# One set of row transposes for the maxima of two head groups in a four-batch decoder layer

## The chip, the cores and the metric

The kernel runs on one core of a Trainium2 chip. Times are device microseconds (us) of that core; lower is better. The engines are TensorE (PE, matrix products and transposes), VectorE (DVE), ScalarE (ACT), GpSimd (POOL) and SyncE (SP, which issues most transfers). They run side by side, each through its own queue in order, and wait for each other through semaphores.

## The reference

A pre-norm decoder layer on x of shape 4 x 512 x 512, all in float32:

```python
x = x + self_attention(layernorm(x))      # 16 heads of 32, causal, q/k/v/o weights and biases
x = x + cross_attention(layernorm(x), ctx) # 16 heads of 32, keys = values = ctx, no weights,
                                           # causal; masked scores are -10000, not -inf
x = x + ffn(layernorm(x))                  # relu(x Wup) Wdown + (sum of softmaxed top-2 gates) * x Wexpert
```

Both attentions are softmax(q k / sqrt(32)) v. In the cross-attention a masked score takes part in the softmax with the value -10000, so that a row whose largest score is far below zero would still weigh the masked keys.

## The kernel before, in words

The four batches are worked one after another; a batch has 512 rows (4 tiles of 128) and 512 columns (4 tiles of 128). The 16 heads stand in four groups `g` = 0 to 3 of four heads, one group per column tile, head `r` of a group on the 32 partitions from 32 `r`. The order of the work on PE, DVE, ACT and POOL is the order in which the program is written (`tc.manual_schedule` with these four engines); only transfers and the constants made before it are placed by the framework. PSUM is one pool of four buffers of two banks, handed out by `pair`.

One attention (class `Attention`, once per batch for self, once for cross) has two passes:

- `with_maxima` computes the scores with the queries on the partitions, only to find each row's largest score. It has ten units (`units`, counted by `n`), and a unit is one or two pieces of a group. Between the units it lays matmuls of other work (`fill`: projections, feed-forward steps). In `maxima`, a unit's scores are copied out of PSUM by ACT (L308), masked by POOL (L316) and reduced by DVE into `nm`, the negated maxima (L328). Group 0 is complete after unit 2, group 1 after unit 4, groups 2 and 3 after units 7 and 9.
- `attend` computes the scores again, transposed (keys on the partitions, L409), adds the negated maximum of each query by a further small matmul (L420), takes the exponential on ACT (L443), masks on POOL (L451) and multiplies by the values (`values`, `shares`, L486). The product of a unit is written two units behind its scores.

The negated maxima have to lie along a row for L420. `split` writes `nm` (128 x 16 for one group: 4 row tiles, 4 heads) as three bfloat16 parts whose sum is the float32 value, into columns 0, 1 and 2 of each head's 32 columns of a tile `parts`; the other columns are zero. `rows` turns `parts` with four TensorE transposes and copies the result to `mrow` (128 x 512, bfloat16). A product with 32 rows of ones (`onesb`) then adds the three parts up:

```python
lhsT=onesb[h, :],
rhs=self.mrow[g][h, j * P :],
```

There are two `parts` tiles, used alternately (`parts[g % 2]`), and one `mrow` for each group. In `with_maxima` the rows of groups 0 and 1 are turned in units 5 and 7; those of the other groups at its end or in `attend` at unit 3 (`late`). In self-attention groups 2 and 3 are both turned at unit 3 of `attend`, into one PSUM buffer (`mt_s_both`), with two copies by ACT.

The cross-attention also needs the weight of the masked keys. `masked_sums` spreads a group's negated maxima over the partitions with one matmul against `same` (a block matrix of ones, L378, tile `mb`). `masked` takes the exponential on ACT (`ct_c`, L385) and returns `weigh`, three steps (L391 to L393) that multiply by the sums of the later keys' values and by the number of later keys. For groups 0 and 1 the products stand in units 6 and 8, and `weigh` runs on POOL, written right after the scores of units 7 and 9; the others come in `attend`.

The constants (identities, ones, zeroed `parts`) are made by POOL at the start, ahead of the POOL steps of the first layer norm (L208, L210).

Of the kernel before, what the change touches and what calls it, by code (L numbers as in the profile page):

```python
# [18 lines left out]
P = 128  # L19
# [7 lines left out]
def decoder_layer(  # L27
# [37 lines left out]
    def pair(name):  # L65

        return ps.tile([P, 2, S], F32, tag="ps", name=name)
# [96 lines left out]
        allow_small_or_imprecise_dtypes=True,  # L164
    )

    nfloor = const.tile([P, NT, HG], F32, name="nfloor")
    nc.gpsimd.memset(nfloor, -MASKED_BIAS)
    nc.gpsimd.affine_select(
# [7 lines left out]
    )  # L177

    parts = []
    for n in range(2):  # L180
        t = const.tile([P, NT, P], BF16, name=f"parts{n}")
        nc.gpsimd.memset(t, 0.0)
        parts.append(t)
# [86 lines left out]
    class Attention:  # L270
        def __init__(self, q_t, k_t, v, cross, name):
            self.q_t, self.k_t, self.v, self.cross, self.name = q_t, k_t, v, cross, name
            self.nm, self.mrow, self.pv, self.out = {}, {}, {}, None
            self.more, self.sums, self.rden, self.e = {}, {}, {}, None
            self.added = (0, 2) if cross else range(NC - 1)

            self.joined = 1 if cross and name != f"c{B - 1}" else None
            self.joint, self.zero = [], None

        def maxima(self, pieces):  # L280

            at, N = [], 0
            for g, i in pieces:
                at.append(N)
                N += (i + 1) * P
                if g not in self.nm:
                    self.nm[g] = small.tile(
                        [P, NT, HG], F32, tag="nm", name=f"nm_{self.name}_{g}"  # L290
                    )
            name = f"{self.name}_{pieces[0][0]}_{pieces[0][1]}"
            scs = [pair(f"sm_{name}_{n}") for n in range(2)]
            for (g, i), c in zip(pieces, at):
                for r in range(HG):
                    h = slice(r * HD, (r + 1) * HD)
                    nc.tensor.matmul(  # L297
                        scs[r // 2][:, r % 2, c : c + (i + 1) * P],
                        lhsT=self.q_t[h, g, i * P : (i + 1) * P],
                        rhs=self.k_t[h, g, : (i + 1) * P],  # L300
                        start=(c == 0),
                        stop=True,
                        skip_group_check=(c > 0),
                    )
            made = []
            for n in range(2):
                s = work.tile([P, 2, S], F32, tag="pt", name=f"s_{name}_{n}", bufs=6)
                nc.scalar.copy(s, scs[n])  # L308

                if len(pieces) == 1:  # L310
                    diagonal = s[:, :, S - P :].unsqueeze(2)
                elif pieces[0][1] == pieces[1][1]:
                    diagonal = s.rearrange("p u (k q) -> p u k q", k=2)[:, :, :, P:]
                else:
                    diagonal = s[:, :, S - 2 * P :].rearrange("p u (k q) -> p u k q", k=2)
                nc.gpsimd.affine_select(  # L316
                    out=diagonal,
                    in_=diagonal,
                    compare_op=ALU.is_ge,
                    fill=NEG,  # L320
                    base=0,
                    pattern=[[0, 2], [0, len(pieces)], [-1, P]],
                    channel_multiplier=1,
                )
                made.append(s)

            def largest(n, g, i, c):
                nc.vector.tensor_reduce(  # L328
                    self.nm[g][:, i, 2 * n : 2 * n + 2],
                    made[n][:, :, c : c + (i + 1) * P],  # L330
                    axis=AX.X,
                    op=ALU.max,
                    negate=True,
                )

            jobs = [
                (lambda n=n, g=g, i=i, c=c: largest(n, g, i, c))
                for n in range(2)
                for (g, i), c in zip(pieces, at)
            ]  # L340
            if pieces == [(pieces[0][0], NT - 1)]:
                jobs.append(lambda: self.split(pieces[0][0]))
            return jobs

        def split(self, g):

            nm, pt = self.nm[g], parts[g % 2].rearrange("p i (r s) -> p i r s", s=HD)
            if self.cross:
                nc.vector.tensor_tensor(nm, nm, nfloor, ALU.min)
            nc.vector.tensor_copy(pt[:, :, :, 0], nm)  # L350
            rest = small.tile([P, NT, HG], F32, tag="rest", name=f"rest_{self.name}_{g}")
            nc.vector.tensor_tensor(rest, nm, pt[:, :, :, 0], ALU.subtract)
            nc.vector.tensor_copy(pt[:, :, :, 1], rest)
            nc.vector.tensor_tensor(pt[:, :, :, 2], rest, pt[:, :, :, 1], ALU.subtract)

        def rows(self, g, both=None, half=0):


            if both is None:
                tp = ps.tile([P, NT, P], BF16, tag="ps", name=f"mt_{self.name}_{g}")  # L360
            else:
                bank = both[:, 0, :].bitcast(BF16)
                tp = bank[:, half * S : (half + 1) * S].rearrange("p (i q) -> p i q", q=P)
            for i in range(NT):
                nc.tensor.transpose(tp[:, i, :], parts[g % 2][:, i, :], identb)
            self.mrow[g] = work.tile(
                [P, S], BF16, tag="mrow", name=f"mrow_{self.name}_{g}", bufs=4
            )

            def copy(engine=nc.vector.tensor_copy):  # L370
                engine(self.mrow[g], tp.rearrange("p i q -> p (i q)"))

            return [copy]

        def masked_sums(self, g, both=None):

            bc = (pair(f"mb_{self.name}_{g}") if both is None else both)[:, 1, :]
            nc.tensor.matmul(bc, lhsT=same, rhs=self.mrow[g], start=True, stop=True)  # L378
            return g, bc

        def masked(self, g, bc):
# [15 lines left out]
        def scores(self, pieces):  # L397
# [19 lines left out]
            for (g, j), c in zip(pieces, at):  # L417
                for r in range(HG):
                    h = slice(r * HD, (r + 1) * HD)
                    nc.tensor.matmul(  # L420
                        scs[r // 2][:, r % 2, c : c + S - j * P],
                        lhsT=onesb[h, :],
                        rhs=self.mrow[g][h, j * P :],
                        start=False,
                        stop=True,
                        skip_group_check=(len(pieces) > 1),
                    )
# [505 lines left out]
    def run(steps):  # L933
        for step in steps:
            for _ in step() or ():
                pass
# [7 lines left out]
    def with_maxima(steps, a, first=0, norms=()):  # L944
# [17 lines left out]
        for n, pieces in enumerate(units):  # L962
            new = a.maxima(pieces)
            if todo:
                todo.pop()(nc.gpsimd)
            if norms and n % 2 == 0:
                new.append(norms.pop(0))
            due += (total - lead) / len(units)

            count = round(due) - done  # L970
            for k in range(count):
                next(fill, None)
                done += 1
                if k == min(1, count - 1) and n in (5, 7):
                    jobs = a.rows((n - 5) // 2) + jobs
                if k == min(1, count - 1) and a.cross and n in (6, 8):
                    todo.append(a.masked(*a.masked_sums((n - 6) // 2)))
                if n == len(units) - 1 and k == count - (2 if count > 4 else 1):
                    if total >= 2 * len(units):
                        if a.cross:  # L980
                            a.rows(2)[0](nc.scalar.copy)
                    else:
                        late = {3: 2, 5: NC - 1}
                run(jobs[:1])
                jobs = jobs[1:]
            run(jobs)
            jobs = new
        for _ in fill:
            pass
        run(jobs)  # L990
        return late

    def attend(a, late):
# [21 lines left out]
        for n, pieces in enumerate(units):  # L1015
            waiting.append(a.scores(pieces))
            if n in late:
                two = a.cross and late[n] == NC - 1
                together = not a.cross and len(late) == 1
                both = pair(f"mt_{a.name}_both") if two or together else None  # L1020
                copies = a.rows(2, both, 1) if together else []
                copies += a.rows(late[n], both)

                more = [a.masked_sums(2, both)] if two else []
                for copy in copies:
# [13 lines left out]
    with tc.manual_schedule(engines=BY_HAND):  # L1039
# [6 lines left out]
        nc.vector.tensor_reduce(  # L1046
            fold, ident.rearrange("p (c e) -> p e c", e=HD), axis=AX.X, op=ALU.add
        )
        add_bias(e)
        between_self = between_self[1:]  # L1050
        skip, between_cross, ahead = 6, [], []
# [102 lines left out]
```

## Time and profile before

| | |
|---|---|
| median of 3 runs | 790.2 us (790.12 to 790.22) |
| profiled execution, whole | 790.27 us |
| its span, first to last instruction | 788.6 us |
| granted TensorE clock | 1.00 |
| HBM traffic | 30 GB/s over the span |
| POOL select L316 behind ACT copy L308, idle | 100.7 us (cross), 90.0 us (self) |
| DVE maximum L328, 128 calls each | 96.7 us (self), 95.9 us (cross) |

The profile is of one execution. The span is what the profiler sees between the first and the last instruction; the time of the run has 1.7 us more around it. Groups of instructions are listed by source line, engine and operation, with their number, busy time and mean length, and with the idle time ahead of them and what ended it. A chain is the sequence of work that ended last, followed back from the end. Busy time of TensorE counts overlapping matmuls once, and the end of each is modelled; what a matmul holds up is better read from the starts of its neighbours.

### The profile page before, as it was taken

To read this page: it belongs to the slowest core of one execution; us is meant where nothing else is said; L and a number is where in the kernel's file an instruction comes from. 1 tells how busy PE (TensorE), PEld (TensorE's weight loads), DVE (VectorE), ACT (ScalarE), POOL (GpSimd) and SP (SyncE) were. 2 spreads that over 40 slices of the span, in tenths; PEclk is the share of its full clock that TensorE was granted. 3 is DMA by queue.
4 is the path that set the end of the run, shared out by engine and by line. 5 is a ranking of instruction groups with operands and counts; after the bars stand their busy time and mean duration, and the time that the engine had idled before them with its cause. 6 is when DMAs were issued, how large, how long until landed. Compare 5 with 4: busy or idle time off the path is not lost.

```text
span 788.6 us, 14119 instructions
## 1 busy us (share of the span) xinstructions
PE 779.9 (99%) x5484; PEld 369.9 (47%) x5488; DVE 584.2 (74%) x991; ACT 381.7 (48%) x436; POOL 339.8 (43%) x523
## 2 busy tenths in 40 slices
PE   8999999999999999999999999999999999999998
PEld 7444444445444444444544444444544444444444
DVE  2488986988678894498767797698859786989512
ACT  2457516871547505666154741787056814774110
POOL 3434612664234741366233482367323653474100
PEclk9999999999999999999999999999999999999999
DMA  8821400001021300030101130000102030000101
GB/s 290 297 47 27 64 2 1 1 29 54 1 46 25 53 14 1 1 108 28 54 17 35 25 62 1 1 1 2 54 27 81 8 48 0 1 2 2 53 1 53
DMA packets 77779, 31.88 MB, mean 40 GB/s; under 512 B 63504, under 2 KB 67856, under 8 KB 77712
## 3 DMA queue, kind: packets, MB, share of 16 engines
q1 hardware_dynamic: 76992, 30.32, 14.5%
q8 instruction: 43, 0.70, 0.3%
q10 hardware_dynamic: 720, 0.66, 0.2%
q14 instruction: 24, 0.20, 0.1%
HBM read 19.42 MB, written 4.19 MB: 30 GB/s over the span
## 4 chain that ended last, share of the span: by engine, by line
PE 93%; DVE 2%; ACT 2%; issue 2%; DMA 0%; POOL 0%; DVEq 0%
PE pm_qk L245 13%; PE pm_d L233 7%; PE pm_u L245 7%; PE pm_v L233 7%; PE pm_o L764 7%; PE pm_e L233 6%; PE pv_s L486 6%; PE pv_c L486 6%; PE sm_c L297 6%; PE sm_s L297 6%; PE sc_s L409 5%; PE sc_c L409 4%; PE sc_s L420 1%; PE sc_c L420 1%; PE pv_s L562 1%
## 5 line engine op out<-in xcount | busy, mean ns | idle before, releaser
L328 DVE TENSOR_REDUCE nm_s<-s_s 128x2 f32<-128x1024 f32 (+3 forms) x128 | 96.7, 809 | 30.0 <-POOL s_s L316 30.0
L328 DVE TENSOR_REDUCE nm_c<-s_c 128x2 f32<-128x1024 f32 (+3 forms) x128 | 95.9, 810 | 31.0 <-POOL s_c L316 31.0
L308 ACT COPY s_s<-sm_s 128x1024 f32<-128x1024 f32 x80 | 77.1, 1015 | 70.7 <-PE sm_s L297 36.4
L308 ACT COPY s_c<-sm_c 128x1024 f32<-128x1024 f32 x80 | 77.1, 1016 | 35.9 <-PE sm_c L297 16.2
L316 POOL TENSOR_SCALAR_AFFINE_SELECT s_c<-s_c 128x512 f32<-128x512 f32 (+1 forms) x80 | 43.9, 550 | 100.7 <-ACT s_c L308 100.7
L316 POOL TENSOR_SCALAR_AFFINE_SELECT s_s<-s_s 128x512 f32<-128x512 f32 (+1 forms) x80 | 43.7, 550 | 90.0 <-ACT s_s L308 90.0
L556 DVE TENSOR_TENSOR sum_s<-sum_s,pt_s 128x256 f32<-128x256 f32 (+2 forms) x72 | 60.0, 898 | 15.4 <-PE pv_s L486 15.4
L443 ACT ACTIVATE pt_c<-sc_c 128x1024 f32<-128x1024 f32 x64 | 61.8, 1031 | 17.2 <-PE sc_c L420 8.7
L451 POOL TENSOR_SCALAR_AFFINE_SELECT pt_c<-pt_c 128x512 f32<-128x512 f32 (+1 forms) x64 | 53.4, 845 | 20.4 <-ACT pt_c L443 20.2
L233 PE MATMUL pm_d<-wdown_sb,hT 128*128 128x512 f32 x128 | 61.5, 610 | 0.0
L245 PE MATMUL pm_u<-fT,wup_sb 128*128 128x512 f32 x128 | 59.3, 604 | 0.0
L443 ACT ACTIVATE pt_s<-sc_s 128x1024 f32<-128x1024 f32 x56 | 53.9, 1029 | 10.5 <-POOL pt_s L451 5.5
L233 PE MATMUL pm_v<-wv_sb,xnT 128*128 128x512 f32 x128 | 58.8, 600 | 0.0
L245 PE MATMUL pm_qk<-xnT,wk_sb 128*128 128x512 f32 x120 | 57.3, 607 | 0.0
L245 PE MATMUL pm_qk<-xnT,wq_sb 128*128 128x512 f32 x120 | 56.7, 604 | 0.0
L233 PE MATMUL pm_e<-wexp_sb,fT 128*128 128x512 f32 x120 | 56.3, 604 | 0.0
L764 PE MATMUL pm_o<-wo_sb,oT_s 128*128 128x512 f32 x128 | 56.0, 595 | 0.0
L451 POOL TENSOR_SCALAR_AFFINE_SELECT pt_s<-pt_s 128x512 f32<-128x512 f32 (+1 forms) x56 | 48.0, 865 | 16.8 <-ACT pt_s L443 16.2
L409 PE MATMUL sc_c<-cqT,ckT 32*128 32x384 f32 (+3 forms) x512 | 54.1, 464 | 0.9 <-ACT sum_c L443 0.8
L409 PE MATMUL sc_s<-qT,kT 32*128 32x128 f32 (+3 forms) x512 | 54.0, 464 | 0.9 <-ACT sum_s L443 0.9
L671 ACT ACTIVATE kT<-pm_qk,bk_sb 128x512 f32<-128x512 f32 x16 | 11.0, 688 | 85.3 <-PE pm_qk L245 80.7
L297 PE MATMUL sm_c<-ckT,cqT 32*128 32x512 f32 (+3 forms) x512 | 47.5, 460 | 0.0
(172 smaller groups left out, 1291.0 us busy)
## 6 DMA issues: line engine op xcount, KB each, us to landing
cv<-in_ctx_dram SPq DMA_DIRECT2D x16, 256.0 KB, 4.2
cp<-cv SPq DMA_DIRECT2D x64, 64.0 KB, 2.3
out_dram<-x SPq DMA_DIRECT2D x15, 256.0 KB, 2.0
xin<-in_x_dram SPq DMA_DIRECT2D x12, 256.0 KB, 2.7
x<-in_x_dram SPq DMA_DIRECT2D x12, 256.0 KB, 4.4
xnT<-xn_a SPq DMA_DIRECT2D x192, 16.0 KB, 1.8
wv_sb<-in_wv_dram SPq DMA_DIRECT2D x1, 1024.0 KB, 8.3
wo_sb<-in_wo_dram SPq DMA_DIRECT2D x1, 1024.0 KB, 9.9
```

Of the source, the lines that this page charges most:

```text
L233: nc.tensor.matmul(pm, lhsT=lhs_t[:, c, t * P : (t + 1) * P], rhs=w[:, c, :], start=(c == 0), stop=(c == NC - 1),)
L245: nc.tensor.matmul(pm, lhsT=w[:, c, f * P : (f + 1) * P], rhs=rhs_t[:, c, :], start=(c == 0), stop=(c == NC - 1),)
L297: nc.tensor.matmul(scs[r // 2][:, r % 2, c : c + (i + 1) * P], lhsT=self.q_t[h, g, i * P : (i + 1) * P], rhs=self.k_t[h, g, : (i + 1) * P] ...
L308: nc.scalar.copy(s, scs[n])
L316: nc.gpsimd.affine_select(out=diagonal, in_=diagonal, compare_op=ALU.is_ge, fill=NEG, base=0, pattern=[[0, 2], [0, len(pieces)], [-1, P]], ...
L328: nc.vector.tensor_reduce(self.nm[g][:, i, 2 * n : 2 * n + 2], made[n][:, :, c : c + (i + 1) * P], axis=AX.X, op=ALU.max, negate=True,)
L409: nc.tensor.matmul(scs[r // 2][:, r % 2, c : c + S - j * P], lhsT=self.k_t[h, g, j * P : (j + 1) * P], rhs=self.q_t[h, g, j * P :], start= ...
L443: nc.scalar.activation(pt, scs[n], AF.Exp)
L451: nc.gpsimd.affine_select(out=diagonal, in_=diagonal, compare_op=ALU.is_ge, fill=0.0, base=0, pattern=[[0, 2], [0, len(pieces)], [1, P]], ...
L486: nc.tensor.matmul(pv[r * HD : (r + 1) * HD, u, j * P :], lhsT=ones if u else self.v[:, j, h * HD : (h + 1) * HD], rhs=pts[r // 2][:, r % ...
L556: nc.vector.tensor_tensor(to, to, pts[n][:, :, c : c + S - j * P], ALU.add)
L764: nc.tensor.matmul(pms[t // 2][:, t % 2, :], lhsT=a.out[:, c, t * P : (t + 1) * P], rhs=wo_sb[:, c, :], start=(c == 0), stop=(c == NC - 1),)
```

## The change

Groups now have homes: in self-attention groups 0 and 1 share one, and groups 2 and 3; in cross-attention groups 0 and 1 share one, and groups 2 and 3 have one each. The groups of a home share an `nm` tile, one `split` (instructions of 32 columns instead of 16), one set of four transposes and one `mrow`. The second group of a home takes columns 3 to 5 of each head's 32. To pick one group's three rows, the matmul of L420 takes `picks[0]` or `picks[1]` instead of `onesb`, and `masked_sums` takes `sames[0]` or `sames[1]` instead of `same`; these are made once by DVE after the first layer norm. There are four `parts` tiles. The rows of groups 0 and 1 are turned in unit 7, and in the cross-attention both their masked products stand together in unit 8, into the two banks of one PSUM buffer. Their two `weigh` steps come after: one behind the scores of unit 9, the other at the end of `with_maxima`.

```diff
-    for n in range(2):
+    for n in range(4):
         t = const.tile([P, NT, P], BF16, name=f"parts{n}")
         nc.gpsimd.memset(t, 0.0)
...
+            homes = [(0, 1), (2,), (3,)] if cross else [(0, 1), (2, 3)]
+            self.home = {
+                g: (gs, 2 + n - 1 if cross and n else n) for n, gs in enumerate(homes) for g in gs
+            }
...
-            if pieces == [(pieces[0][0], NT - 1)]:
-                jobs.append(lambda: self.split(pieces[0][0]))
+            g = pieces[0][0]
+            if pieces == [(g, NT - 1)] and g == self.home[g][0][-1]:
+                jobs.append(lambda: self.split(g))
...
         def split(self, g):
+            gs, at = self.home[g]
+            N = len(gs)
+            pt = parts[at].rearrange("p i (r s) -> p i r s", s=HD)
+            pt = [pt[:, :, :, k : 3 * N : 3] for k in range(3)]
...
+            nc.vector.tensor_copy(pt[0], nm)
+            nc.vector.tensor_tensor(rest, nm, pt[0], ALU.subtract)
+            nc.vector.tensor_copy(pt[1], rest)
+            nc.vector.tensor_tensor(pt[2], rest, pt[1], ALU.subtract)
...
-            nc.tensor.matmul(bc, lhsT=same, rhs=self.mrow[g], start=True, stop=True)
+            nc.tensor.matmul(bc, lhsT=sames[self.slot(g)], rhs=self.mrow[g], start=True, stop=True)
...
-                        lhsT=onesb[h, :],
+                        lhsT=picks[self.slot(g)][h, :],
...
             if todo:
-                todo.pop()(nc.gpsimd)
+                todo.pop(0)(nc.gpsimd)
...
-                if k == min(1, count - 1) and n in (5, 7):
-                    jobs = a.rows((n - 5) // 2) + jobs
-                if k == min(1, count - 1) and a.cross and n in (6, 8):
-                    todo.append(a.masked(*a.masked_sums((n - 6) // 2)))
+                if k == min(1, count - 1) and n == 7:
+                    jobs = a.rows(0) + jobs
+                if k == min(1, count - 1) and a.cross and n == 8:
+                    both = pair(f"mb_{a.name}_both")
+                    sums = [a.masked_sums(g, both, g) for g in range(2)]
+                    todo.extend(a.masked(*each) for each in sums)
...
         run(jobs)
+        for weigh in todo:
+            weigh(nc.gpsimd)
         return late
...
-                together = not a.cross and len(late) == 1
-                both = pair(f"mt_{a.name}_both") if two or together else None
-                copies = a.rows(2, both, 1) if together else []
-                copies += a.rows(late[n], both)
+                both = pair(f"mt_{a.name}_both") if two else None
+                copies = a.rows(late[n], both)
...
+        nc.vector.tensor_reduce(
+            slots, fold[:, :6].rearrange("p (g k) -> p g k", k=3), axis=AX.X, op=ALU.add
+        )
+        for n in range(2):
+            nc.vector.tensor_scalar(picks[n], onesb, slots[:, n : n + 1], None, ALU.mult)
+            nc.vector.tensor_scalar(sames[n], same, slots[:, n : n + 1], None, ALU.mult)
```

More of the change, by code (lines that the diff above doesn't have):

```diff
@@ L165, in decoder_layer @@
     )
+    picks = [const.tile([P, P], BF16, name=f"pick{n}") for n in range(2)]
+    sames = [const.tile([P, P], BF16, name=f"same{n}") for n in range(2)]
+    slots = const.tile([P, 2], F32, name="slots")
     nfloor = const.tile([P, NT, HG], F32, name="nfloor")
@@ L288, in maxima @@
                 if g not in self.nm:
-                    self.nm[g] = small.tile(
-                        [P, NT, HG], F32, tag="nm", name=f"nm_{self.name}_{g}"
-                    )
+                    nm = small.tile([P, 2, NT, HG], F32, tag="nm", name=f"nm_{self.name}_{g}")
+                    for k, other in enumerate(self.home[g][0]):
+                        self.nm[other] = nm[:, k]
+                    self.nm[self.home[g][0]] = nm
             name = f"{self.name}_{pieces[0][0]}_{pieces[0][1]}"
@@ L340, in maxima, with rows @@
             ]
-            if pieces == [(pieces[0][0], NT - 1)]:
-                jobs.append(lambda: self.split(pieces[0][0]))
+            g = pieces[0][0]
+            if pieces == [(g, NT - 1)] and g == self.home[g][0][-1]:
+                jobs.append(lambda: self.split(g))
             return jobs
         def split(self, g):
-            nm, pt = self.nm[g], parts[g % 2].rearrange("p i (r s) -> p i r s", s=HD)
-            if self.cross:
[L349 to L356, printed above, removed]
+            gs, at = self.home[g]
+            N = len(gs)
+            pt = parts[at].rearrange("p i (r s) -> p i r s", s=HD)
+            pt = [pt[:, :, :, k : 3 * N : 3] for k in range(3)]
+            nm = self.nm[gs][:, :N]
+            rest = small.tile([P, 2, NT, HG], F32, tag="rest", name=f"rest_{self.name}_{g}")
+            rest = rest[:, :N].rearrange("p g i r -> p i r g")
+            if self.cross:
+                nc.vector.tensor_tensor(
+                    nm, nm, nfloor.unsqueeze(1).to_broadcast([P, N, NT, HG]), ALU.min
+                )
+            nm = nm.rearrange("p g i r -> p i r g")
+            nc.vector.tensor_copy(pt[0], nm)
+            nc.vector.tensor_tensor(rest, nm, pt[0], ALU.subtract)
+            nc.vector.tensor_copy(pt[1], rest)
+            nc.vector.tensor_tensor(pt[2], rest, pt[1], ALU.subtract)
+        def rows(self, g, both=None):
+            gs, at = self.home[g]
             if both is None:
@@ L362, in rows, with slot, masked_sums @@
                 bank = both[:, 0, :].bitcast(BF16)
-                tp = bank[:, half * S : (half + 1) * S].rearrange("p (i q) -> p i q", q=P)
+                tp = bank[:, :S].rearrange("p (i q) -> p i q", q=P)
             for i in range(NT):
[L365 to L368, printed above, removed]
+                nc.tensor.transpose(tp[:, i, :], parts[at][:, i, :], identb)
+            row = work.tile([P, S], BF16, tag="mrow", name=f"mrow_{self.name}_{g}", bufs=4)
+            for other in gs:
+                self.mrow[other] = row
             def copy(engine=nc.vector.tensor_copy):
-                engine(self.mrow[g], tp.rearrange("p i q -> p (i q)"))
+                engine(row, tp.rearrange("p i q -> p (i q)"))
             return [copy]
-        def masked_sums(self, g, both=None):
-            bc = (pair(f"mb_{self.name}_{g}") if both is None else both)[:, 1, :]
-            nc.tensor.matmul(bc, lhsT=same, rhs=self.mrow[g], start=True, stop=True)
+        def slot(self, g):
+            return self.home[g][0].index(g)
+        def masked_sums(self, g, both=None, bank=1):
+            bc = (pair(f"mb_{self.name}_{g}") if both is None else both)[:, bank, :]
+            nc.tensor.matmul(bc, lhsT=sames[self.slot(g)], rhs=self.mrow[g], start=True, stop=True)
             return g, bc
@@ L1048, in decoder_layer @@
         )
+        nc.vector.tensor_reduce(
+            slots, fold[:, :6].rearrange("p (g k) -> p g k", k=3), axis=AX.X, op=ALU.add
+        )
+        for n in range(2):
+            nc.vector.tensor_scalar(picks[n], onesb, slots[:, n : n + 1], None, ALU.mult)
+            nc.vector.tensor_scalar(sames[n], same, slots[:, n : n + 1], None, ALU.mult)
         add_bias(e)
```

## The prediction

> **What bounds the kernel now.** I read the page's first and fourth parts first. In the page, the busy times and the chain by engine:
>
> ```profile
> PE 779.9 (99%) x5484; PEld 369.9 (47%) x5488; DVE 584.2 (74%) x991; ACT 381.7 (48%) x436; POOL 339.8 (43%) x523
> PE 93%; DVE 2%; ACT 2%; issue 2%; DMA 0%; POOL 0%; DVEq 0%
> ```
>
> TensorE sets the time: a matmul taken out of its queue is worth its place in the queue, and a wait put into that queue costs its length. POOL, at 43%, looks harmless, but that is a mean; what counts is where each POOL result is due. Next, the groups by line for PE, the row transposes that the change thins out:
>
> ```profile
> L365 PE MATMUL mt_c<-identb,parts 128*128 128x128 bf16 x48 | 4.6, 219 | 0.0
> L365 PE MATMUL mt_s<-identb,parts 128*128 128x128 bf16 x32 | 3.1, 219 | 0.0
> L365 PE MATMUL mt_s_both<-identb,parts 128*128 128x128 bf16 x32 | 2.5, 220 | 0.0
> ```
>
> Their 219 ns is a latency; matmuls overlap. What a set costs is read in the chain in order of time (start, length, what), here around the first self-attention:
>
> ```profile
> 47.62 0.22 PE mt_s L365 x4
> 49.84 2.77 PE pm_v L233 x6
> 71.82 0.55 PE mt_s_both L365 x8
> ```
>
> Four transposes hold the queue for 0.22 us, eight for 0.55. Last, the timeline at the end of the first cross-attention's maxima pass (its `with_maxima`), where the POOL work is moved:
>
> ```profile
> 151.51 0.42 POOL L316 TENSOR_SCALAR_AFFINE_SELECT s_c<-s_c 128x256 f32<-128x256 f32 x1 [0.49 <-ACT s_c L308]
> 151.88 0.10 POOL L391 MEMSET ct_c<- 128x1 f32 x1
> 152.06 1.27 POOL L392 TENSOR_TENSOR behT<-ct_c,behT 128x512 f32<-128x512 f32 x1
> 153.41 1.27 POOL L393 TENSOR_TENSOR ct_c<-ct_c,cnt 128x512 f32<-128x512 f32 x1
> 154.63 0.82 POOL L451 TENSOR_SCALAR_AFFINE_SELECT sum_c<-sum_c 128x256 f32<-128x256 f32 x2
> 156.31 1.06 PE L486 MATMUL pv_c<-sum_c,cv 128*32 128x512 f32 x8
> ```
>
> Group 1's weighing (L391 to L393) fills POOL from 151.88 to 154.63, 2.75 us. The two selects behind it finish at 155.45, and TensorE reads their result at 156.31: 0.86 us to spare. The change puts group 0's weighing in front of the same selects.
>
> **Self-attention.** Four sets of transposes become two. The set in unit 5 goes: the stretch 45.71 to 48.76 (3.05 us) holds six pm_v matmuls with the set, and six without one take 2.77 (49.84), so 0.28; in the last batch the set lies between pm_e and the next maxima and costs 0.22. At unit 3 of `attend`, eight transposes become four: half of 0.55, 0.27. Per batch 0.5 to 0.55, over four batches -2.15. ACT loses one 0.59 copy per batch there; the exponentials behind it wait 0.33 for PE in the trace (at 74.91), so this is worth nothing.
>
> The remaining set at unit 3 waits for the last split, now of two groups. In the trace that split ends at 71.45 and the transposes start at 71.82 with no wait in the chain, so some 0.3 us is free. DVE reaches it at the same time as before, because the addition at 64.47 waits for TensorE's last pm_v (64.43). Its four instructions grow from 16 to 32 columns. Nearest rows: a reciprocal of 128x4 takes 178 ns and of 128x16 254 ns, so 16 more columns add about 0.1 each at most, 0.4 in all; the low bound is nothing. I take nothing, because 254 ns against 178 is already mostly fixed cost; twice the duration of all four (1.63 us here) would make a 1.3 us wait per batch and is left to the tail.
>
> **Cross-attention, TensorE.** One set goes from unit 5: 0.22. The product of group 0 (mb, 0.22 in the chain) moves from unit 6 to unit 8 and is only moved. So TensorE reaches the end of unit 8 0.22 early. The transposes at unit 7 now need both groups' splits: group 1's split ended at 141.94 and its set was loaded at 144.34, 2.4 us of cover, and DVE meanwhile has one split and one row copy less.
>
> **Cross-attention, POOL.** In the first batch, with the shift of -0.22, the last s_c select ends at 151.71. Weighing 0 then runs from 151.66, weighing 1 from 154.41, and the two selects of sum_c from 157.16, ending at 157.57 and 157.98. The first four-head product pv_c, due at 156.09, can start two heads after the first select and the other two after the second. Counting 0.07 from POOL to PE, its last heads start at 158.05 against 156.31 before: +1.74, and +1.34 if only the first select counted. Behind the waiting product stands TensorE's whole queue; ACT, already fed with units 1 and 2, runs on. That gives something back: the next scores (chain 157.37 to 159.11, 1.74 us) wait for ACT to free a PSUM buffer, while the same form unhindered takes 1.29 (77.00), so 0.45 returns. Net +1.3, with 0.85 and 1.74 as ends. ACT itself has both ct_c exponentials together, which just fits (free at about 149.25, its next copy due at 149.30).
> - Third batch: the same pattern (select 524.34, product 529.14): +1.3.
> - Second batch: eight pm_e matmuls stand between the maxima and the scores. Last select ending 343.62, weighing 343.57 to 346.37, product at 349.57. Two weighings end at 348.95 and the selects at 349.36 and 349.77: between -0.22 and +0.27, and the 0.45 is there to absorb it. I take -0.1.
> - Fourth batch: ACT is late in unit 8, so the two ct_c together push the copies of unit 9 by 0.3. Memset 690.97 becomes 691.25, two blocks of 2.82 (690.97 to 693.79) end at 696.9, the selects at 697.7, product before at 695.81: +1.96, less 0.45, +1.5 (ends 1.0 and 2.0).
>
> Sum of the four, TensorE's 0.22 included: +4.0. The later products are not hit: their POOL selects (0.64 each) are caught up by about 161, and TensorE asks for the first of them at about 161 too, the others later.
>
> **Start.** `parts` grows from two tiles to four, so POOL clears two more before the layer norm's first POOL step:
>
> ```profile
> 4.13 0.53 POOL L182 MEMSET parts<- 128x512 bf16 x1
> 4.79 0.22 POOL L208 TENSOR_SCALAR ve_a<-mv_a 128x1 f32<-128x1 f32 x1
> 5.09 0.57 POOL L210 TENSOR_TENSOR rs_a<-ve_a,mhalf 128x1 f32<-128x1 f32 x1
> ```
>
> These POOL steps are in the chain that releases TensorE's first matmuls (8.63). Two memsets of about 0.5 less 0.13 idle: +0.87 (0.5 if they overlap more, 1.06 in full). The reduction and the four scalings that make the picking matrices fall into DVE's 17.26 us of idle time before the first maximum; without that cover they would cost about 2 us once (five at 0.4, by fold's 375 ns). LDWEIGHTS of pick instead of onesb have the same form: nothing.
>
> **Sum.** -2.15 + 4.0 + 0.87 = +2.7. The profiled execution took 790.27 (span 788.6 and 1.7 around it), the median is 790.2; so 793.0. A difference of 0.2%, 1.6 us, is about what a measurement of this kernel can tell from none.
>
> [...] The transposes: the rows give 0.055 us each in the queue, 2.6 for the 48 removed. [...] I go by the chain, in which four take 0.22. [...]
>
> **Rivals.**
> - TensorE's stream alone decides (not slower). If the late selects were covered, the sum is -2.15 - 0.88 + 0.87 = -2.2: 788.1. In the first batch this needs a weighing of at most 1.77 us ((156.02 - 151.66 - 0.82) / 2), where the rows show 2.75; over the kernel the sign turns once the four crosses together cost less than 1.28. For it: the page's POOL at 43%, and TensorE never waited for POOL there before. Against it: an order on POOL that is fixed by the program. 0.12.
> - A wash: POOL delays at their low ends (0.85, 0.85, -0.22, 1.0), start at 0.5: +0.8, so 791.0. 0.17.
> - The POOL block slows DVE and itself: casts and sums of DVE contend with it (three selects took 3.27 at 158.70 where they take 0.64 alone), the wider split makes TensorE wait at unit 3, and nothing is given back: crosses +6.9 and splits +0.5: 796.4. 0.08.
> - That the change does not do what it says is excluded: in the order of the built program 20 sets of transposes are left of 32, two per self-attention and three per cross-attention, and POOL's order is the one used above.
>
> **How the numbers follow.** The forecast itself holds 0.63. The range leaves out the first rival and the last, 0.20 together. Its low end is the wash less 0.06 (the spread between 0.28 and 0.22) on each of the eight sets taken out of self-attention, 790.5. Its high end is every cross at its upper end (1.74, 0.27, 1.74, 2.0: 5.75) with the start at 1.06, so +4.7, 795.0. Faster by over 0.2% is the first rival, 0.12; within 0.2% the wash and a sliver of the forecast, 0.18; slower 0.70.
>
> **What would show it.** Right: mt_s 32 and mt_c 48 (with mt_c_both) instead of 64 and 64; sum_c selects starting about 5.5 us after the last s_c select; a new wait of pv_c on POOL's sum_c of 1 to 2 us in batches one, three and four, none in the second; ve_a at about 5.7. Wrong: these products start without a wait, or a wait of mt_s_3 on DVE's parts.

## The result and the profile after

| | before | after |
|---|---|---|
| median | 790.21 us (790.12 to 790.23) | 795.99 us (793.65 to 796.60) |
| profiled execution, whole | 790.27 us | 796.60 us |
| its span | 788.6 us | 794.8 us |
| granted TensorE clock, mean | 1.00 | 0.996 |

The change makes the kernel slower: the ratio is 1.0068, with a 95% interval of 1.0047 to 1.0089. The forecast was 793.0, its range 790.5 to 795.0: the direction is right, the time lies above the range. The kernel before repeats within 0.11 us, the changed one doesn't: its four runs took 796.60, 793.65, 796.51 and 795.46, and only the run of 793.65 had a granted clock of 1.00. Where these 3 us come from is the main question below.

First the page, its busy times and its chain by engine:

```profile
PE 780.4 (98%) x5440; PEld 367.5 (46%) x5440; DVE 573.5 (72%) x936; ACT 378.6 (48%) x432; POOL 335.9 (42%) x525
PE 90%; POOL 3%; ACT 2%; DVE 2%; issue 1%; ACTq 0%; POOLq 0%; DVEq 0%
```

POOL does less than before (335.9 us for 339.8) and yet has a place in the chain, 3% instead of 0%. DVE has 55 instructions fewer, PE's weight loads 48. The work went down as intended; the end moved for another reason. The groups by line show that the transposes are the fewer that were meant:

```profile
L383 PE MATMUL mt_s<-identb,parts 128*128 128x128 bf16 x32 | 3.1, 220 | 0.0
L383 PE MATMUL mt_c<-identb,parts 128*128 128x128 bf16 x32 | 3.1, 219 | 0.0
L383 PE MATMUL mt_c_both<-identb,parts 128*128 128x128 bf16 x16 | 1.6, 222 | 0.1
```

The waits of TensorE have one new leader (total, times, longest, in us):

```profile
PE pv_c L507 <- POOL sum_c L472: 4.7, 3, 1.7
```

And the timeline shows POOL and TensorE where the first cross-attention passes from `with_maxima` to `attend`, the place that was shown of before:

```profile
151.83 0.42 POOL L325 TENSOR_SCALAR_AFFINE_SELECT s_c<-s_c 128x256 f32<-128x256 f32 x1 [0.49 <-ACT s_c L317]
152.20 0.10 POOL L412 MEMSET ct_c<- 128x1 f32 x1
...
154.95 0.09 POOL L412 MEMSET ct_c<- 128x1 f32 x1
...
157.71 0.79 POOL L472 TENSOR_SCALAR_AFFINE_SELECT sum_c<-sum_c 128x256 f32<-128x256 f32 x2
158.18 2.30 PE L507 MATMUL pv_c<-sum_c,cv 128*32 128x512 f32 x8 [1.52 <-POOL sum_c L472]
```

Two weighings stand back to back, from 152.20 to 157.71, or 5.51 us; the selects of `sum_c` come behind them, and TensorE waits 1.52 us. So far this is the forecast. What the forecast doesn't have is the length in the last line: these eight products take 2.30 us, where the same eight took 1.06 before, and 1.43 in batch 4 of this profile, where the second half of them waits for the second select, as the forecast counts it. The stretches of the profile tell why; the column before the last two is the granted TensorE clock:

```profile
core 0: us, PE busy (x) PEld busy (x) DVE busy (x) ACT busy (x) POOL busy (x), PEclk, DMA share, GB/s
156.00:157.00 1.00, 0.66 (x15) 0.23 (x6) 0.93 (x3) 1.00 (x3) 0.92 (x2) 1.00 0.00 0
157.00:158.00 1.00, 0.00 (x0) 0.00 (x0) 0.96 (x2) 1.00 (x3) 1.00 (x2) 0.98 0.00 0
158.00:159.00 1.00, 0.82 (x4) 0.37 (x8) 0.55 (x2) 0.91 (x1) 1.00 (x3) 0.50 0.00 0
...
161.00:162.00 1.00, 1.00 (x12) 0.10 (x4) 1.00 (x3) 0.00 (x0) 0.00 (x0) 0.82 0.00 0
...
533.42:536.83 3.41, 3.41 (x16) 0.87 (x16) 2.07 (x4) 0.34 (x1) 2.49 (x4) 0.50 0.02 5
...
702.00:704.00 2.00, 1.76 (x12) 0.60 (x16) 1.90 (x5) 0.81 (x1) 2.00 (x5) 1.00 0.03 8
```

TensorE stands still for about 1.5 us, its clock falls to half, and it stays there after the work is back, for some 3.4 us (about 157.9 to 161.4). In batch 3 the same happens from 533.42 to 536.83; there the clock falls 0.38 us after the products have begun at 533.04. In batch 4 the wait is 1.69 us, the longest, and the clock stays at 1.00 (last row, which lies behind the wait). So 1.5 us of standing still was enough for the half clock in two places, and 1.69 us did not bring it on in a third.

### The profile page after: what moved, and what is told of

Its sections match the earlier page's. It is cut to its first block, busy times and chain, and to the rows that moved or that the text cites. A ratio compares the mean times of both kernels' runs of the same rounds, so it can differ in the third digit from the quotient of the medians.

```text
span 794.8 us, 13965 instructions
## 1 busy us (share of the span) xinstructions
PE 780.4 (98%) x5440; PEld 367.5 (46%) x5440; DVE 573.5 (72%) x936; ACT 378.6 (48%) x432; POOL 335.9 (42%) x525
## 4 chain that ended last, share of the span: by engine, by line
PE 90%; POOL 3%; ACT 2%; DVE 2%; issue 1%; ACTq 0%; POOLq 0%; DVEq 0%
PE pm_qk L249 13%; PE pm_u L249 7%; PE pm_v L237 7%; PE pm_o L785 7%; PE pv_c L507 7%; PE pm_e L237 7%; PE pm_d L237 6%; PE sm_s L306 6%; PE pv_s L507 5%; PE sm_c L306 5%; PE sc_s L430 5%; PE sc_c L430 4%; PE sc_s L441 1%; ACT sum_s L464 1%; DVE nm_c L337 1%
## 5 line engine op out<-in xcount | busy, mean ns | idle before, releaser
L472 POOL TENSOR_SCALAR_AFFINE_SELECT pt_c<-pt_c 128x512 f32<-128x512 f32 (+1 forms) x64 | 48.5, 774 | 23.7 <-ACT pt_c L464 23.5
```

Source lines behind the costliest of these rows:

```text
L472: nc.gpsimd.affine_select(out=diagonal, in_=diagonal, compare_op=ALU.is_ge, fill=0.0, base=0, pattern=[[0, 2], [0, len(pieces)], [1, P]], ...
```

## The theory and its rivals

Theory: the cross-attention loses through POOL's order alone, that is through the wait and the half clock that the wait sometimes brings on. Rivals: the wait costs what it is long, and the spread has another cause; the longer POOL block costs through DVE, whose additions and splits run slower beside it; the pairing itself (wider splits, later sets) costs something. Separately, the self-attention should have gained 2.15 us and shows about half of that.

## The experiments

**The second weighing, later.** The weighing of group 1 leaves the end of the maxima pass and goes behind unit 2 of `attend`.

```diff
         run(jobs)
-        for weigh in todo:
-            weigh(nc.gpsimd)
+        a.put = todo
         return late
...
+            if n == 2 and a.put:
+                a.put.pop()(nc.gpsimd)
             if n in (3, 4) and put_off:
```

> The changed kernel with one thing different: the second weighing (POOL, 2.75 us) is issued behind the selects of unit 2 of attend instead of ahead of all of attend's selects. Theory (late selects, and the half clock that their wait brings on): the waits of pv_c on POOL's sum_c (4.7 us) go, the granted clock stays at 1.00, and what is left is +0.77 at the start, -0.28, -0.28, -0.28 and -0.22 in self-attention and -0.22 four times in cross-attention: -1.2, so 789.0, with a spread of the runs of 0.1 to 0.2. Rival (the wider splits beside POOL, or the paired ct_c on ACT, hold TensorE up): most of the +5.8 stays, 793 to 796.

Measured 794.45 us (794.43 to 795.96), ratio 1.0063 [1.0050, 1.0077]: a miss by more than 5 us. The wait for POOL at the first `pv_c` is gone, but another is in its place, and the weighing has become slower. TensorE's waits over the whole kernel, then DVE's and POOL's rows of the timeline in batch 1:

```profile
PE pv_c L583 <- DVE sum_c L577: 1.9, 2, 1.3
```

```profile
157.75 6.77 DVE L577 TENSOR_TENSOR sum_c<-sum_c,pt_c 128x256 f32<-128x256 f32 x6 [0.80 <-PE pv_c L507]
...
160.46 1.81 POOL L413 TENSOR_TENSOR behT<-ct_c,behT 128x512 f32<-128x512 f32 x1
...
162.35 1.61 POOL L414 TENSOR_TENSOR ct_c<-ct_c,cnt 128x512 f32<-128x512 f32 x1
```

Moved there, the weighing lies beside DVE's six additions. They take 6.77 us instead of 5.04, the weighing's two steps 1.81 and 1.61 instead of 1.27 each, and TensorE needs those sums at once. The two waits in the first row are batch 4's; in batch 1 the products of the sums aren't put down as waiting, but take 2.22 us instead of 1.04. By the starts of TensorE's later instructions the cross-attention takes about 0.8 us more than before in each of the first three batches and 1.9 in the last. The second rival is a real effect, though not the one that the changed kernel suffers from. Two of the five runs also took 1.5 us more, at a clock of 0.997.

**The gap filled with useless work.** POOL's order is left as it is; TensorE gets seven products whose results nobody reads (14 in the trace, where each stands twice), to pass the time of the wait.

```diff
                 self.pv[g] = pair(f"pv_{self.name}_{g}")
+                if self.cross and g == 0 and self.name != "c1":
+                    for _ in range(7):
+                        nc.tensor.matmul(
+                            self.pv[g][:, 1, :P], lhsT=ident, rhs=ident, start=True, stop=True
+                        )
```

> The changed kernel with seven matmuls of 128 columns without use ahead of the first product pv_c of the cross-attentions of batches one, three and four, written into a half of its PSUM buffer that is written over later. They fill some 1.5 us of the wait and shorten nothing. Theory (the half clock follows TensorE's gap): the granted clock stays at 1.00, the product takes about 1.4 us as in the fourth batch instead of 2.3, every run lies near the fastest of the changed kernel, 793.7, with a spread under 0.5, against 793.65 to 796.6. Rival (the clock falls for another reason, or falls at random): median 795 to 796.6 and a clock below 1.00 as before, or slower by the 3 x 1.5 us of the matmuls.

Measured 793.72 us (793.62 to 793.86), ratio 1.0045 [1.0032, 1.0057]. More work, and the kernel is 2.3 us faster than the changed one by the medians; the spread shrinks from 2.95 to 0.24 us, and all clocks are 1.00. The product of the sums starts late as before, but takes 1.29 us instead of 2.30:

```profile
156.57 1.83 PE L500 MATMUL pv_c<-ident 128*128 128x128 f32 x14
158.33 1.29 PE L512 MATMUL pv_c<-sum_c,cv 128*32 128x512 f32 x8
159.55 1.14 PE L430 MATMUL sc_c<-cqT,ckT 32*128 32x512 f32 x8
```

This is the experiment that sizes the missing term. Against it the changed kernel's profiled execution is 796.60 - 793.72 = 2.9 us longer; by batches its crosses cost 2.78 and 3.10 us in batches 1 and 3, those of this kernel 1.47 and 1.47, so the half clock took 1.3 and 1.6.

**Half of the filler.** Three useless products instead of seven.

> e2_warm_gap with three useless products in the gap ahead of the first pv_c instead of seven, about 0.6 us of work, so that some 0.9 us of the gap stays. Theory A (the low clock comes only with a gap near 1.5 us): all runs near 793.7 us, clock 1.00. Theory B (any gap of about 1 us can bring it on): the runs spread as those of the changed kernel do, 793.7 to 796.6 us, with half clock for some 3.4 us in the disturbed ones. The wait itself stays in either case, since POOL's work is the same.

Measured 793.85 us (793.71 to 795.52), ratio 1.0051 [1.0037, 1.0065]. The wait left to TensorE is 0.66 us in batch 1. Four of five runs lie with those of the full filler; one took 795.52 at a clock of 0.998. Neither theory holds cleanly: a gap of under 1 us mostly leaves the clock alone, but one run in five did see a low clock, and no profile shows where in it.

**Only POOL's order.** The kernel before, without any pairing; only its weighings are issued where the changed kernel has them.

```diff
-            if todo:
-                todo.pop()(nc.gpsimd)
+            if todo and n == 9:
+                todo.pop(0)(nc.gpsimd)
...
         run(jobs)
+        for weigh in todo:
+            weigh(nc.gpsimd)
         return late
```

> The kernel before with POOL's order alone changed: the weighing of group 0 in the cross-attention is issued behind the scores of unit 9 instead of unit 7, that of group 1 right after it. Transposes, products, exponentials and copies are those of before. Theory: the late selects with their clock are the whole loss, so waits of 1.5 to 1.9 us in batches one, three and four, a granted clock of 0.996 in most runs, and +4.5 to +7: 795 to 797. Rival (the loss comes from the pairing: wider splits, shared rows, two exponentials in a row): within 1 us of 790.2.

Measured 795.98 us (794.56 to 796.20), ratio 1.0067 [1.0055, 1.0080]. The wait of `pv_c` for POOL's `sum_c` is 4.1 us in three places, and the two runs at a clock of 1.00 took 794.6, the three at 0.998 took 796.0 to 796.2: one half clock more or less is 1.5 us. So the order on POOL alone, with nothing else changed, makes the whole loss; what else the change does comes to about 1 us of gain (793.65 against 794.6, both at full clock).

**Only the self-attention.** Paired sets in the self-attention, the cross-attention as before, two `parts` tiles.

```diff
...
-            homes = [(0, 1), (2,), (3,)] if cross else [(0, 1), (2, 3)]
+            homes = [(0,), (1,), (2,), (3,)] if cross else [(0, 1), (2, 3)]
...
```

> The pairing in self-attention alone: cross-attention with a split, a set of transposes and a product for each group and POOL's order as before; two parts tiles, so nothing is added at the start. Theory (the set taken out at unit 3 is given back in a wait for ACT, as the scores behind it take 1.72 us instead of 1.49): 0.28, 0.28, 0.28 and 0.22, so -1.06: 789.15. The prediction's term: -2.15: 788.05. Rival (the pairing itself costs): at or above 790.2.

Measured 789.08 us (789.02 to 789.45), ratio 0.9987 [0.9978, 0.9996]: 1.1 us gained where the prediction's term was 2.15.

**The self-attention with its set at unit 3 issued twice.** The last kernel with the transposes that the pairing saved at unit 3 put back.

```diff
-            for i in range(NT):
+            for i in [*range(NT)] * (2 if not self.cross and g == NC - 1 else 1):
                 nc.tensor.transpose(tp[:, i, :], parts[at][:, i, :], identb)
```

> e4_self_only (only the self-attention paired, 789.1 us) with the remaining set of four transposes at unit 3 of the second pass issued twice, eight transposes as in the kernel before. Theory (what is saved there is given back at once, since the scores behind it wait for ACT to free their PSUM buffer): no change, 789.1 us, within 0.2 us. Rival (TensorE's queue counts there, as the prediction had it): four sets more at 0.22 to 0.27 us, 790.0 to 790.2 us.

Measured 789.14 us (789.06 to 789.27), ratio 0.9986 [0.9977, 0.9994]. Four sets more, 0.06 us more: what is saved at unit 3 is worth nothing. The reason stands in the timeline, in the weight loads of the scores behind the set, first in the changed kernel, then in this one:

```profile
73.58 0.30 PEld L430 LDWEIGHTS sc_s<-qT,kT 32*128 32x128 f32 x4 [0.62 <-ACT sum_s L464]
...
74.16 0.52 PEld L430 LDWEIGHTS sc_s<-qT,kT 32*128 32x128 f32 x12 [0.28 <-ACT sum_s L464]
```

```profile
72.93 0.88 PEld L428 LDWEIGHTS sc_s<-qT,kT 32*128 32x128 f32 x16 [0.62 <-ACT sum_s L462]
```

With four transposes the scores begin earlier and stop after the first four loads until ACT has read the other half of its PSUM buffer; with eight they run through. The next exponential starts 3.16 us behind the set's start in both (72.25 to 75.41 and 71.38 to 74.54).

**The first weighing, earlier.** It is issued ahead of the last unit's scores instead of behind them, into time in which POOL is idle.

```diff
         for n, pieces in enumerate(units):
-            new = a.maxima(pieces)
             if todo:
                 todo.pop(0)(nc.gpsimd)
+            new = a.maxima(pieces)
```

> The changed kernel with POOL's first weighing issued ahead of the scores of the last unit of the maxima pass instead of behind them, so that it falls into time in which POOL is idle; the second stays at the end of the pass. Theory (what the cross-attention lost was POOL's order alone, with the half clock that its wait brings on): only one weighing, 2.75 us, then stands between the last s_c select and the sum_c selects, as in the kernel before; pv_c waits at most 0.1 us for POOL in each batch, the clock stays at 1.00, and the time is 790.2 - 1.1 (self-attention alone, as measured) - 0.9 (TensorE's sets in the cross-attention) + 0.8 (start) = 789.0 us. Rival (the weighing pushes the last unit's selects, and with them the last maxima and split, or slows DVE on the way): 791 us or more, with a new wait of TensorE for DVE's maxima or split.

Measured 793.73 us (793.70 to 793.79), ratio 1.0044 [1.0031, 1.0056]: the rival. POOL's selects are in time now, and the first `pv_c` of batch 1 doesn't wait. But TensorE waits for DVE's `parts` (3.0 us in two places, batches 1 and 3) and in one place for its `sum_c` (1.6, batch 4). DVE's split of group 2, and what POOL does at that time:

```profile
149.70 1.25 DVE L369 CAST parts<-nm_c 128x16 bf16<-128x16 f32 x1
150.99 1.29 DVE L370 TENSOR_TENSOR rest_c<-nm_c,parts 128x16 f32<-128x16 f32 x1
```

```profile
149.62 1.27 POOL L413 TENSOR_TENSOR behT<-ct_c,behT 128x512 f32<-128x512 f32 x1
150.97 1.27 POOL L414 TENSOR_TENSOR ct_c<-ct_c,cnt 128x512 f32<-128x512 f32 x1
```

In the changed kernel the same cast and subtraction take 0.20 and 0.18 us. Here each begins just behind the start of a POOL step of 1.27 us (0.08 and 0.02 us) and ends just behind its end (0.06 and 0.04 us): the two DVE instructions last as long as the POOL step beside them. Also to be noted: the profile has three waits of about 1.5 us on TensorE (1.49, 1.49 and 1.58), and in none of the five runs was the clock below 1.00.

**The second weighing, later still.** As in the first experiment, but behind unit 4 of `attend`, two units later.

```diff
...
+            if n == 4 and a.put:
+                a.put.pop()(nc.gpsimd)
```

> The changed kernel with POOL's second weighing put behind the scores of unit 4 of the second pass, two units later than in e1_weigh_late. Theory (e1 failed because the weighing fell beside DVE's additions to the sum_c tiles that TensorE was waiting for): where DVE's work is not due at once the same instructions cost nothing, pv_c waits for neither POOL nor DVE, and the time is 789.0 us by the same sum as for f1_gap. Rival (a late weighing slows DVE or the later selects of POOL wherever it stands in the second pass): 792 us or more, with a wait of pv_c for DVE or POOL above 1 us.

Measured 788.90 us (788.87 to 788.98), ratio 0.9983 [0.9974, 0.9992], as expected. The sum's product runs on time, and the weighing's two steps take 1.28 us each, for 1.27 in the kernel before:

```profile
156.60 1.06 PE L507 MATMUL pv_c<-sum_c,cv 128*32 128x512 f32 x8
...
165.31 1.28 POOL L413 TENSOR_TENSOR behT<-ct_c,behT 128x512 f32<-128x512 f32 x1
166.67 1.28 POOL L414 TENSOR_TENSOR ct_c<-ct_c,cnt 128x512 f32<-128x512 f32 x1
```

**The added memsets, later.** The earlier weighing of `f1_gap`, and the two new `parts` tiles cleared behind the first layer norm.

```diff
-        nc.gpsimd.memset(t, 0.0)
+        if n < 2:
+            nc.gpsimd.memset(t, 0.0)
...
         nc.gpsimd.tensor_scalar(bqs_sb, bq_sb, SCALE, None, ALU.mult)
+        for t in parts[2:]:
+            nc.gpsimd.memset(t, 0.0)
```

> f1_gap with the two added memsets of parts moved behind the first layer norm. Theory: they lay in the chain that releases TensorE's first matmul, so the first pm_qk starts at 8.6 us instead of 9.4 and the time is 0.8 us under f1_gap, about 788.2 us. Rival (the start is covered by a later wait, such as that for the first weights or the first scores): no difference from f1_gap beyond 0.2 us.

Measured 793.02 us (792.76 to 793.14), ratio 1.0034 [1.0021, 1.0048]: 0.71 less than `f1_gap`, and the first pm_qk starts at 8.57 instead of 9.40. The start term is real and can be had back; the absolute time is off by what `f1_gap` was off.

**Both repairs.** `f2_unit4` with the later memsets.

> f2_unit4 with the two added memsets of parts moved behind the first layer norm, as in f3_gap_start: all parts that the runs found good together. Theory (the two terms lie in different stages and add up): 788.9 - 0.7 = 788.2 us, the clock at 1.00 throughout, and no wait of pv_c for POOL or DVE. Rival (a gain at the start is taken back by a later wait): 788.9 us.

Measured 788.00 us (787.96 to 788.37), ratio 0.9973 [0.9962, 0.9983] against the kernel before: the fastest of all, 2.1 us under before and 8.0 under the change as made. POOL is at 0% of its chain again:

```profile
PE 95%; ACT 3%; issue 1%; DVE 0%; POOL 0%; ACTq 0%; POOLq 0%
```

## Why the prediction was right and wrong

The step that failed is the price of the wait in the cross-attention. The prediction took a wait to cost its length, "a wait put into that queue costs its length", less 0.45 that comes back. It left out that TensorE may run at half clock after standing still. That term measured 1.3 us in batch 1 and 1.6 in batch 3 of the profiled run, 2.9 together, and none in the run of 793.65 and in the filled kernel. A second, smaller failure stands in the self-attention: 1.09 us were counted as a gain that didn't come. At full clock it is partly hidden, because the crosses cost 0.45 and the start 0.10 less than forecast; that 793.65 lies so near 793.0 is in part luck.

Term by term, by the starts of the same instructions in the traces; the middle column is the kernel with the filled gap, that is the change at full clock:

| term, us | predicted | full clock | after |
|---|---|---|---|
| start, two more memsets | +0.87 | +0.77 | +0.77 |
| self-attention, four batches | -2.15 | -1.06 | -1.06 |
| cross, batch 1 | +1.3 | +1.47 | +2.78 |
| cross, batch 2 | -0.1 | -0.24 | -0.23 |
| cross, batch 3 | +1.3 | +1.47 | +3.10 |
| cross, batch 4 | +1.5 | +0.85 | +0.85 |
| sum | +2.7 | +3.3 | +6.2 |

- The start: right in place and nearly in size; moving the memsets gave 0.71 back.
- Self-attention, the set in unit 5: right. Its 0.28, 0.28, 0.28 and 0.22 are the whole measured gain of 1.06.
- Self-attention, the set at unit 3: wrong. Here 0.27 a batch, 1.09 in all, was counted as a gain. The prediction read the set in TensorE's queue and asked only whether ACT's copy mattered, not whether the scores behind the set had a buffer to write to. They had not: ACT sets the pace there, and `e5_self_eight` shows that the four sets can come back for nothing.
- The transposes: the four sets taken out of unit 5 gave 1.06, or 0.066 us for each of 16 transposes, near the chain's 0.055.
- The wider split, taken at nothing: its four instructions took 1.53 us for 32 columns in the first batch, the same as the 1.53 for 16 columns before, and no `mt_s` waited for it.
- POOL in the cross-attention: right. The waits were to be 1 to 2 us in batches one, three and four and none in the second; they were 1.52, 1.53, 1.69 and none. In batch 1 the selects were to start at 157.16; they started at 157.71, or at 157.20 once the 0.51 that the batch came late is taken off. In the kernel with half the filler, at full clock, the product starts 1.36 later than that lateness and takes 1.43 instead of 1.06: +1.73 at its end, where the prediction had 1.74. Of this 0.27 comes back behind it, not 0.45. (The prediction's low end of 0.85 for this batch is 0.89 by its own numbers, 1.34 less 0.45.) At full clock the crosses cost 3.55 together, the forecast 4.0.
- Batch 4: mis-sized. ACT was to push the last select by 0.28; less the 5.39 that the batch came late, the memset behind it lies at 690.83, against 690.97 before, so the delay didn't come. The product starts 1.04 later and the net is 0.85 at full clock, where the prediction had 1.96 and 1.5.
- DVE beside POOL: the forecast's sum has no term for it. In the kernel before, group 3's second cast, 0.20 us for the first, took 0.67 beside a POOL select of 0.64 (155.98 and 155.95). In the changed kernel group 3's split, beside the longer POOL block, ended at 158.6, or 158.1 without the 0.51 of lateness. Two of its five instructions took 1.18 and 1.10 us and ended 0.03 and 0.04 us behind POOL's steps of 1.27 and 1.29; the other three took 0.20 to 0.37. No cost followed; in `f1_gap`, where TensorE needed the split of group 2 at once, it was late beside POOL and cost 1.49 us at two places.
- The first rival, a gain when the late selects are covered, was priced at 788.1. With POOL's order repaired (`f2_unit4`) the time is 788.9; the difference is less than the 1.09 of the set at unit 3.

By this account the change at full clock is worth +3.3 us, 793.5 against a forecast of 793.0. The upper end of 795.0 left no room for the clock, and the third rival's 796.4, with a 6.9 for the crosses that the prediction doesn't derive, comes near the time with the wrong mechanism: DVE's slowing beside POOL is real (six additions in 6.77 us instead of 5.04 in `e1_weigh_late`), but it isn't what this kernel paid for.

Left open: why a gap of 1.5 us brings the half clock on in some places and runs and not in others. It came in batches 1 and 3 of the profiled run and not in batch 4 with the longer wait, in three of four runs of the changed kernel, in three of five of `e3_order_only`, and in none of the five of `f1_gap`, whose three waits come right behind 128-row products instead of scores of 32 rows. The trace of the changed kernel narrows it down in one way: the changes of its clock lie on a grid of 3.41 us. The two falls lie 375.47 us apart (157.95 and 533.42), which is 110 times 3.413, and each lasts one step; the full clock recorded ahead of the first lasts from 4.35 to 157.95, 153.60 us or 45 steps. The gaps of batches 1, 3 and 4 each lie in one step, but for 0.23 us at most, and TensorE was busy for 1.90, 1.72 and 1.84 of that step's 3.41 us (from 154.54, 530.00 and 700.67); for the three of `f1_gap` it is, as an estimate, 1.92, 1.92 and 1.83 (3.41 less the waits of 1.49, 1.49 and 1.58, if each lies in one step). So neither the length of the gap nor TensorE's busy time in the step tells the two falls from the rest. Whether the work before the gap does, or chance, nothing here separates.

## What to carry to other kernels

When steps of an engine that is mostly idle are put together, ask what stands behind them in its queue, and price the wait that follows with the clock that TensorE may lose by it (here 1.3 and 1.6 us on waits of 1.5); filling the gap with useless products tells in one run how much of a loss is wait and how much is clock. A step that POOL can take late is to be put where DVE has nothing due: the same three steps behind unit 4 instead of unit 2 made the kernel 5.5 us faster (788.90 for 794.45), by their place alone. And a matmul taken out of TensorE's queue only counts if the next one has a buffer to write to: here four sets of four transposes, put back in `e5_self_eight`, cost 0.06 us.

## What the runs showed of the hardware

- In two places of the changed kernel's profile a standstill of TensorE of 1.5 us was followed by half its clock for 3.41 us, which cost 1.3 and 1.6 us more than the wait; in a third, of 1.69 us, the clock stayed at 1.00. In the times alone it shows as a spread between runs (793.65 to 796.60), so a kernel whose runs spread more than its neighbours' deserves a look at the clock by stretches.
- A DVE cast of 128x16, 0.20 us in the changed kernel, took 1.25 us beside a POOL step of 1.27 us in `f1_gap`; in `e1_weigh_late` six DVE additions took 6.77 us instead of 5.04 beside two POOL steps, which themselves took 1.81 and 1.61 instead of 1.27.
- In the changed kernel's profile the granted clock changed at steps of 3.41 us: it was half from 157.95 to 161.36 and from 533.42 to 536.83, 110 steps apart.
